# Order of the reflections, of the residual sum and of two late pieces in a fused attention, expert and rotation kernel

## The chip, the cores and the metric

One Trainium2 chip, and on it one core. The core has five engines that run beside each other, each through its own list of instructions in order: TensorE (PE in the profile; its weight loads are PEld), VectorE (DVE), ScalarE (ACT), GpSimd (POOL) and SyncE (SP). Work passes between them by semaphores. The kernel uses SP and POOL to issue most of its DMA transfers, and an issue waits in the list of its engine like any other instruction; a sequencer's own part of an engine is marked with a q (SPq, POOLq).

The metric is the device time of one launch in microseconds. Before the change three runs gave 720.19, 721.65 and 724.29 us; the median, 721.65 us, is what a ratio is taken to.

## The reference

The input is x of 4 batches of 512 tokens with 288 channels, and one condition vector for each batch. All arithmetic is float32.

```python
mod = silu(c) @ w_adaln + b_adaln           # six vectors of 288 for each batch
h   = layernorm(x) * (1 + sc_msa) + sh_msa
o   = attention(h, 16 heads of 18)          # 512 x 512 scores in each head
x   = x + g_msa * (o @ w_proj + b_proj)
xn  = layernorm(x) * (1 + sc_mlp) + sh_mlp
cw  = softmax weights of the best 2 of 4 experts, by xn @ w_gate
moe = sum_e cw[e] * (gelu(xn @ w1[e] + b1[e]) @ w2[e] + b2[e])      # 1152 hidden
x   = x + g_mlp * moe
U, _ = qr(P)                                # P: 288 x 64
R   = expm(A(c))                            # a 64 x 64 rotation for each batch
out = x + ((x @ U) @ R - x @ U) @ U.T
```

## The kernel before, in words

Tokens lie on the 128 partitions, so a batch is 4 tiles of 128 tokens. The program has two large stages and a short end.

**Attention, in 64 steps.** The heads go in groups of four; a step is one group and one tile of 128 keys. The groups of all batches are numbered n = 0 to 15 (batch n // 4, group g = n % 4), and a step is written (g, t). In each step TensorE makes the scores `z` (L1780), ScalarE takes their exponential `es` (L1789), and TensorE multiplies the exponentials of the step before with the values into `av` (L1798). All the rest of the work is cut into pieces, and a dictionary `steps[g, t]` names by hand the pieces that follow the scores of each step. The list `beside` gives one more piece to each step, from the matrices of the rotation. The pieces that matter here:

- *Normalisation of a group n*, in four pieces: `first` copies `av` to `oraw` on ScalarE (L1815) and has SP bring the softmax sums to `den` (L1818); `reciprocals` inverts them on VectorE (L1824) and has SP write them to memory as `rdr` (L1826); `spread` has SP load them back, one row for 32 partitions, into the tile `oT` (L1834); `divide` multiplies `oraw` by `oT` on VectorE (L1840). Below, "den(14)" and the like mean such a piece of group 14.
- *`merge` of a batch*, one piece for each token tile: TensorE multiplies `oT` by the projection into `po` (L1856), VectorE multiplies it by a gate into `og` (L1865), and GpSimd adds `og` to the tile of x, `xs` (L1866). It runs during the next batch, in the steps (1,1) and (1,2).
- *`statistics`* (L1167 to L1176): mean and variance of each token on VectorE, and then on GpSimd the factor `rs`, the power -1/2 of variance + eps, and `ms` = -mean * rs. `normalized` applies both on ScalarE (`xh`, L1184).
- *`routing` of a batch* starts after its merge, in the step (1,3) of the next batch, with the statistics. Its pieces are `norm` (`xh` on ScalarE), `logits0` and `logits1` (VectorE: modulation, L1882 and L1883, and the gate logits, L1930), `top` and `choices` (the best two experts, VectorE), `ratio` (an exponential, ScalarE) and `gates_`. After batches 1 and 3, that is when half of the tokens are known, the pieces `ranks_of`, `by_rank` and `slots_of` give each token its slots, and GpSimd writes the rows there by 16 indirect transfers (`slots`, L2119), which are issued one after the other between other pieces.
- *A column*: one of the 64 reflections of the QR of P. All of it is VectorE work: some 20 small instructions which each need the one before (L1541 to L1605), so about 5 us. A piece `column` takes the next of the list `chain` (a first step, 64 columns, and `ws`, which ends the list). The columns are told apart below by the width that they still have: the column of 267, of 266 and so on.

**Experts, in 108 steps.** The tokens are taken in two halves, each with four passes (one expert each). A pass loads its rows from the slots (`xg`), turns them, multiplies them by the first weights (`ph`, L2443 and L2456), takes the gelu (`hm`, L2465), multiplies by the second weights (`pe`, L2503), and has GpSimd scatter the result into `chosen` (L2519). The list `rest` gives one piece to each step. It opens with `last_merge`, the division of the groups 14 and 15 and the merge of batch 3; then come the routing of batch 3 and the columns that are left; later `turned` and the other pieces that make the basis U (`pwt`, L1625, is the first TensorE work that needs the last column), and the sums of the first half. At the second piece of each pass the program also issues the next pass's `xg` on SP (L2175 to L2180), and it does so ahead of the piece of that step.

**The end.** The sums of the second half, the projection on U, the rotation and the store, in a pipeline over pairs of tiles.

What sets the order: each engine's list is the order in which the Python program issues its instructions, and SP's and POOL's transfers stand in these lists too. PSUM tiles for side work come in turn from three buffers in the attention stage (two of `ps_m`, one of `third`), and from two after it; a piece that is late in emptying its buffer holds up the third, or second, piece after it on TensorE.

Of the kernel before, what the change touches and what calls it, by code (L numbers as in the profile page):

```python
# [10 lines left out]
F32 = mybir.dt.float32  # L11
I32 = mybir.dt.int32
AF = mybir.ActivationFunctionType
ALU = mybir.AluOpType
# [4 lines left out]
P = 128  # L19
HD = 18  # L20
HQ = 32
LN_EPS = 1e-6
# [791 lines left out]
def fast_path(  # L814
# [24 lines left out]
    nc = tc.nc  # L839
    B, N, C = x.shape  # L840
    CC = C // 3
    NK = 3
    NT = N // P
# [97 lines left out]
    def bank(shape, name):  # L941

        banks[0] += 1
        if third and banks[0] % 3 == 0:
            return third[0].tile(shape, F32, tag="n", name=name)
        return ps_m.tile(shape, F32, tag="m", name=name)
# [3 lines left out]
    small = ctx.enter_context(tc.tile_pool(name="small", bufs=4))  # L950
# [6 lines left out]
    with ExitStack() as s1:  # L957
# [204 lines left out]
        def statistics(b, which):  # L1162
            st = small.tile([P, NT, 6], F32, tag="st", name=f"st{which}{b}")
            mv = small.tile([P, NT, 2], F32, tag="mv", name=f"mv{which}{b}")
            rs = small.tile([P, NT], F32, tag="rs", name=f"rs{which}{b}")
            for t in range(NT):
                nc.vector.bn_stats(st[:, t, :], xs[:, b * NT + t, :])  # L1167
                nc.vector.bn_aggr(mv[:, t, :], st[:, t, :])
            nc.gpsimd.tensor_scalar_add(rs, mv[:, :, 1], LN_EPS)
            nc.gpsimd.tensor_tensor(rs, rs, neghalf, ALU.pow)  # L1170
            if (b, which) != (0, 0):

                ms = small.tile([P, NT], F32, tag="ms", name=f"ms{which}{b}")
                nc.gpsimd.tensor_tensor(ms, mv[:, :, 0], rs, ALU.mult)
                nc.gpsimd.tensor_scalar_mul(ms, ms, -1.0)
                return ms, rs  # L1176
            return mv, rs

# [673 lines left out]
        def merge(b):  # L1852
            def tile_of(t):
                po = bank([P, C], f"po{b}{t}")
                for g in range(NG):
                    nc.tensor.matmul(  # L1856
                        po,
                        oTs[b][:, g, ts(t, P)],
                        wp[:, g, :],
                        start=(g == 0),  # L1860
                        stop=(g == NG - 1),
                    )
                xt = xs[:, b * NT + t, :]
                og = small.tile([P, C], F32, tag="og", name=f"og{b}{t}", bufs=2)
                nc.vector.tensor_mul(og, po, gates[:, 0, b, :])  # L1865
                nc.gpsimd.tensor_tensor(xt, xt, og, ALU.add)  # L1866

            return [lambda t=t: tile_of(t) for t in range(NT)]

        def route(b):  # L1870

            xr = rt.tile([P, NT, ROW], F32, tag="xr", name=f"xr{b}", bufs=B // HALVES)
            parts = statistics(b, 1)

            xhs_ = []

            def norm():
                xhs_.append(normalized(b, 1, *parts))

            def modulated(t):  # L1880
                xh = xhs_[0]
                nc.vector.tensor_mul(xh[:, t, :], xh[:, t, :], modrow[:, 1, b, :])  # L1882
                nc.vector.tensor_add(xr[:, t, :C], xh[:, t, :], modrow[:, 0, b, :])  # L1883

            def with_logits(i, logits):
                for t in range(i * NT // 2, (i + 1) * NT // 2):
                    modulated(t)
                logits()

            chosen_ = choose(b, xr)  # L1890
            for i in range(2):
                chosen_[i] = lambda i=i, logits=chosen_[i]: with_logits(i, logits)
            return [norm] + chosen_
# [5 lines left out]
        def scatter_next():  # L1899
            if scatters:  # L1900
                scatters.pop(0)()
# [242 lines left out]
        NN = B * NG  # L2144
        norm, turns, values = begin(0)
# [103 lines left out]
        chain, basis = triangular()  # L2249
        held, divides, late = [], {}, []  # L2250

        def gather_oldest():
            n, t, es = held.pop(0)
            gather(n, t, es)
            if t == NT - 1:
                first, *divides[n] = normalize(n)
                first()

        def divide(n):
            if n in divides:  # L2260
                divides[n].pop(0)()
# [4 lines left out]
        def also(step, *pieces):  # L2266
            steps[step].extend(pieces)

        def routing(b):
            def start():  # L2270
                norm, logits0, logits1, top, choices, ratio, gates_, *end = route(b)
                also((2, 1), norm)
                also((2, 2), logits0)
                also((2, 3), logits1)
                if b == B - 2:

                    also((3, 0), top, choices)
                    also((3, 3), ratio)
                    late.append(gates_)
                    return  # L2280
                also((3, 0), top, choices)
                also((3, 1), ratio)
                also((3, 2), gates_, *end[:1])
                also((3, 3), *end[1:])

            return start
# [14 lines left out]
        for n in range(NN):  # L2301
            b, g = divmod(n, NG)
            if g == 0:
                steps = {(i, t): [] for i in range(NG) for t in range(NT)}
                for i in range(NG):
                    also((i, 0), lambda n=n + i - 2: divide(n))
                    for t in (2, 3):
                        also((i, t), lambda n=n + i - 1: divide(n))
                if b > 0:
                    merges = merge(b - 1)  # L2310
                    also((1, 1), *merges[:2])
                    also((1, 2), *merges[2:])
                    also((1, 3), routing(b - 1))
                else:

                    for step in ((1, 0), (1, 3), (2, 1), (2, 3)):
                        also(step, column)
                if b + 1 < B:
                    also((1, 1), beginning(b + 1))
                if b > 0:  # L2320
                    also((0, 2), column)
                if b == B - 1:
                    also((2, 0), column)
                for step in ((0, 0), (0, 1), (0, 3), (3, 1)):
                    also(step, column)
                also((2, 3), lambda b=b: residual(b))
            if g == 0:
                queue = nc.gpsimd if b else nc.sync
                products, sends = project(b, 1, queue)
                also((0, 0), products[0])  # L2330
                also((0, 1), products[1])
                also((0, 2), *sends[:3])
                also((0, 3), *sends[3:5])
                also((1, 0), *sends[5:])
                products, sends = project(b, 2, queue)
                also((0, 2), *products)
                also((0, 3), sends[0])
                also((1, 1), sends[1])
            if g == 3 and b + 1 < B:
                products, sends = project(b + 1, 0)  # L2340
                also((3, 0), products[0])
                also((3, 1), products[1])
                also((3, 2), *sends[:4])
                also((3, 3), *sends[4:])
            if n == NN - 1:
                wx = wxs[0]
                weights = [expert_weights(0)]
                takes = take_slots(0, xg0)
                also((3, 2), *takes[:3])
                also((3, 3), *takes[3:])  # L2350
            for t in range(NT):
                if (n, t) == (NN - 2, 0):

                    xg0 = load_slots(0, a2, "hT", 1, nc.gpsimd)
                held.append((n, t, weigh(n, t)))
                if len(held) > 1:
                    gather_oldest()
                for piece in steps[g, t]:
                    piece()
                if beside:  # L2360
                    beside.pop(0)()
                scatter_next()
                if g in (0, 1, 3):
                    scatter_next()
        while held:
            gather_oldest()
        for piece in beside:
            piece()
        last_merge = [
            lambda: (divide(NN - 2), divide(NN - 1)),  # L2370
            lambda: divide(NN - 1),
            column,
            lambda: divide(NN - 1),
            None,
            *merge(B - 1),
            *late,
        ]
# [4 lines left out]
    with ExitStack() as s2:  # L2382
# [148 lines left out]
        class Finish:  # L2531
# [6 lines left out]
            late = []  # L2538
# [137 lines left out]


        ROUTING = 13
        rest = [*last_merge, last_routing] + [column] * (len(chain) - 4)
        ends = basis + [None, all_fit, subspace, None] + [  # L2680
            lambda n=n: early(n) for n in range(PAIRS + 1)
        ] + [None] * 4
        steps = HALVES * (E * NF + SLOTS // P)
# [131 lines left out]
```

## Time and profile before

The profiled execution took 724.75 us, 3.10 us more than the median of the three runs; its span from the first to the last instruction is 723.0 us.

| engine | busy, us | share of the span | instructions |
|---|---|---|---|
| PE (TensorE matmul) | 674.6 | 93% | 3563 |
| PEld (weight load) | 391.4 | 54% | 3563 |
| DVE (VectorE) | 485.3 | 67% | 2204 |
| ACT (ScalarE) | 290.2 | 40% | 465 |
| POOL (GpSimd) | 223.3 | 31% | 350 |

| stretch of the span, us | PE busy | DVE busy | POOL busy | granted clock of TensorE |
|---|---|---|---|---|
| 0 to 60 | 52.83 | 35.42 | 21.80 | 1.00 |
| 60 to 120 | 52.83 | 38.66 | 31.78 | 0.91 |
| 120 to 180 | 56.63 | 44.61 | 15.61 | 0.97 |
| 180 to 240 | 56.03 | 48.24 | 17.39 | 1.00 |
| 240 to 300 | 52.84 | 40.40 | 32.84 | 0.97 |
| 300 to 360 | 51.77 | 28.66 | 11.77 | 0.89 |
| 360 to 420 | 60.00 | 48.90 | 19.43 | 1.00 |
| 420 to 600 (mean of 60) | 59.85 | 53.29 | 18.71 | 1.00 |
| 600 to 660 | 58.13 | 13.66 | 12.59 | 1.00 |
| 660 to 720 | 53.95 | 26.85 | 3.97 | 0.94 |

How to read it: the attention stage ends near 319 us, and the expert stage runs from there to 691 us. TensorE is hardly ever idle in the expert stage; its idle time, 48.4 us in all, lies in the attention stage, about the change of stage, and at both ends. A busy share is an average, so the question for each edit is which single wait of TensorE it touches.

### The profile page before, as it was taken

Reading aid. Unit: us, or ns where it says so; the run is one execution under the profiler, and the core shown is the slowest. Engines: PE = TensorE matmul, PEld = TensorE weight load, DVE = VectorE, ACT = ScalarE, POOL = GpSimd, SP = SyncE. Lnnn points to the kernel's source line nnn. Section 1 sums busy time; section 2 is a strip of 40 time slices with the busy share of each in tenths; the row PEclk is TensorE's granted clock in tenths of the full one; section 3 lists DMA queues with packets and bytes.
Section 4 is the critical chain, followed back from the end, with each engine's and each line's share of the span. In section 5 each row is a group of like instructions: output and inputs, shape, how many; then the busy total and the mean of one; then the engine's idle time right before and its main releaser. Section 6 shows DMA issues by size and latency. Waiting matters only on the chain. (4 is left out here: it accounts for less than half of the span.)

```text
span 723.0 us, 11477 instructions
## 1 busy us (share of the span) xinstructions
PE 674.6 (93%) x3563; PEld 391.4 (54%) x3563; DVE 485.3 (67%) x2204; ACT 290.2 (40%) x465; POOL 223.3 (31%) x350
## 2 busy tenths in 40 slices
PE   6999699999998999596999999999999999999986
PEld 5423333333343434143677776777667676667753
DVE  5473868696868883873178788988888886005244
ACT  3566455575547554462224323223232332222231
POOL 3055922601252346720142163622204032121110
PEclk9999899999999999799899999999999999999997
DMA  9488812001100123425143543255343053206043
GB/s 208 137 242 205 283 46 53 21 17 46 49 20 17 54 79 92 138 55 156 60 120 68 171 121 121 73 153 173 75 145 90 12 174 76 90 22 217 18 157 122
DMA packets 70528, 75.47 MB, mean 104 GB/s; under 512 B 33452, under 2 KB 57746, under 8 KB 70458
## 3 DMA queue, kind: packets, MB, share of 16 engines
q1 hardware_dynamic: 60166, 47.78, 24.1%
q0 software_dynamic: 9792, 26.45, 12.1%
q10 hardware_dynamic: 500, 0.42, 0.3%
q8 instruction: 30, 0.49, 0.3%
q14 instruction: 40, 0.33, 0.2%
HBM read 52.13 MB, written 18.23 MB: 97 GB/s over the span
## 5 line engine op out<-in xcount | busy, mean ns | idle before, releaser
L2503 PE MATMUL pe<-w2s,hm 128*128 128x288 f32 (+1 forms) x648 | 163.7, 408 | 0.0
L2443 PE MATMUL ph<-xgT,w1s 128*128 128x288 f32 (+2 forms) x576 | 152.9, 416 | 0.4
L1789 ACT ACTIVATE es<-z 128x1024 f32<-128x1024 f32 x128 | 123.9, 1020 | 69.8 <-PE z L1780 68.1
L2503 PEld LDWEIGHTS pe<-w2s,hm 128*128 128x128 f32 (+1 forms) x648 | 118.7, 187 | 31.5 <-issue 2.3
L2443 PEld LDWEIGHTS ph<-xgT,w1s 128*128 128x128 f32 x576 | 106.8, 191 | 40.5 <-issue 11.4
L2465 ACT ACTIVATE hm<-ph,b1r 128x576 f32<-128x576 f32 (+2 forms) x72 | 49.9, 738 | 140.0 <-PE ph L2456 121.6
L1780 PE MATMUL z<-qk 32*128 32x512 f32 x512 | 90.7, 650 | 14.1 <-ACT es L1789 14.1
L1798 PE MATMUL av<-es,vt 128*32 128x512 f32 x512 | 70.8, 626 | 0.0
L2518 POOL TENSOR_TENSOR y<-y,gb 128x288 f32<-128x288 f32 x32 | 26.1, 816 | 126.6 <-ACT y L2517 126.5
L1780 PEld LDWEIGHTS z<-qk 32*128 32x128 f32 x512 | 27.3, 186 | 58.9 <-ACT es L1789 43.4
L2517 ACT ACTIVATE y<-pe,weight 128x288 f32<-128x288 f32 x32 | 16.0, 501 | 104.2 <-PE pe L2503 100.8
L1742 PE MATMUL pq<-hT,wqk 96*126 96x512 f32 (+3 forms) x120 | 56.5, 608 | 0.0
L2519 POOL DMA_INDIRECT chosen<-y,place x36 | 36.7, 1019 | 53.0 <-DVE y L2515 34.3
L1562 DVE SCALAR_TENSOR_TENSOR q<-q 64x1 f32<-64x1 f32 (+1 forms) x192 | 44.3, 231 | 7.0
L2119 POOL DMA_INDIRECT slots<-xr,where x32 | 32.6, 1017 | 47.4 <-DMA slots<-xr,where 38.8
L1754 POOL DMA_DIRECT2D qk<-row x42 | 21.6, 519 | 72.5 <-ACT row L1749 72.4
L1856 PE MATMUL po<-wp,oT 128*128 128x288 f32 x128 | 35.0, 421 | 9.2 <-DVE oT L1840 9.2
L1573 DVE STREAM_SHUFFLE wj<-pt 32x288 f32<-32x288 f32 (+47 forms) x96 | 42.1, 439 | 0.7
L1742 PEld LDWEIGHTS pq<-hT,wqk 96*126 96x126 f32 (+3 forms) x120 | 20.7, 183 | 33.8 <-issue 28.9
L1798 PEld LDWEIGHTS av<-es,vt 128*32 128x32 f32 x512 | 10.2, 109 | 48.8 <-issue 40.3
L1856 PEld LDWEIGHTS po<-wp,oT 128*128 128x128 f32 x128 | 23.5, 191 | 22.4 <-DVE oT L1840 10.6
L1840 DVE TENSOR_TENSOR oT<-oraw,oT 128x512 f32<-128x512 f32 x16 | 11.0, 689 | 34.3 <-DMA oT<-rdr 28.0
(281 smaller groups left out, 895.6 us busy)
## 6 DMA issues: line engine op xcount, KB each, us to landing
w2s<-in_w_dram SPq DMA_DIRECT2D x8, 1296.0 KB
w1s<-in_w_dram SPq DMA_DIRECT2D x8, 1152.0 KB
slots<-empty POOLq DMA_DIRECT2D x36, 148.0 KB
oT<-rdr SPq DMA_DIRECT2D x64, 64.0 KB
qk<-row POOLq DMA_DIRECT2D x42, 72.0 KB
yc<-chosen SPq DMA_DIRECT2D x4, 576.0 KB
out_dram<-xs SPq DMA_DIRECT2D x8, 288.0 KB
wr<-in_wrT_dram POOLq DMA_DIRECT2D x4, 567.0 KB
```

Source lines behind the costliest of these rows:

```text
L1562: nc.vector.scalar_tensor_tensor(s, u, part, s, ALU.mult, ALU.add)
L1573: nc.vector.stream_shuffle(wj[o : o + HQ, j:], pt[o0 : o0 + HQ, j:], [j % HQ] * HQ)
L1742: nc.tensor.matmul(pq[:n], wqk[:rows, k, item, :n], hT[:rows, k, :], start=(k == 0), stop=(k == NK - 1),)
L1780: nc.tensor.matmul(zs[c // 2][:, c % 2, :], qk[ts(c, HQ), 1, ts(t, P)], qk[ts(c, HQ), 0, :], start=True, stop=True,)
L1789: nc.scalar.activation(e, z, AF.Exp, scale=SCALE)
L1798: nc.tensor.matmul(avs[n][ts(c, HQ), :], vts[b % 2][:, t, 4 * g + c, :], es[c // 2][:, c % 2, :], start=(t == 0), stop=(t == NT - 1),)
L1856: nc.tensor.matmul(po, oTs[b][:, g, ts(t, P)], wp[:, g, :], start=(g == 0), stop=(g == NG - 1),)
L2119: nc.gpsimd.indirect_dma_start(out=slots[h], out_offset=bass.IndirectOffsetOnAxis(ap=where[:, i, t : t + 1], axis=0), in_=xrs[t // NT][:, ...
L2443: nc.tensor.matmul(ph[:, j, :SB], w1s[:, k, ts(f, P)], xgT[:, k, ts(j, SB)], start=(k == 0), stop=False,)
L2465: nc.scalar.activation(hm[:, f, : CAPS[r]].rearrange("p (j s) -> p j s", j=NB), ph[:, :, :SB], AF.Gelu_apprx_tanh, bias=b1r[:, h, r, f : f ...
L2503: nc.tensor.matmul(po[ts(m, rows), :], slots_[:, f, :], w[:, f, :], start=(f == 0), stop=(f == NF - 1),)
L2519: nc.gpsimd.indirect_dma_start(out=chosen[h], out_offset=bass.IndirectOffsetOnAxis(ap=place[:, t : t + 1], axis=0), in_=y, in_offset=None, ...
```

## The change

- The columns of a step are issued last in it, after the step's other pieces and after the piece of `beside`. Before, they stood among the other pieces, and ahead of `beside`.
- The merge's sum `xs + og` is made on VectorE and no longer on GpSimd.
- `statistics`: variance + eps and the negated mean are made on VectorE, the power and one product stay on GpSimd; before, all four were on GpSimd.
- The routing of batch 2, which runs in the steps of batch 3: `norm` moves from the step (2,1) to (2,2), `logits0` from (2,2) to (2,3), `logits1` from (2,3) to (3,0), and `top` with `choices` from (3,0) to (3,1); `ratio` stays in (3,3).
- `last_merge`, the first ten pieces of the expert stage: the three pieces with divisions move from the places 0, 1 and 3 to the places 1, 2 and 3; the column of place 2 moves to place 0, and a second column takes place 4, which was empty. One column fewer is left for later.

```diff
-            nc.gpsimd.tensor_scalar_add(rs, mv[:, :, 1], LN_EPS)
+            nc.vector.tensor_scalar_add(rs, mv[:, :, 1], LN_EPS)
+            if (b, which) != (0, 0):
+                ms = small.tile([P, NT], F32, tag="ms", name=f"ms{which}{b}")
+                nc.vector.tensor_scalar_mul(ms, mv[:, :, 0], -1.0)
             nc.gpsimd.tensor_tensor(rs, rs, neghalf, ALU.pow)
             if (b, which) != (0, 0):
-                ms = small.tile([P, NT], F32, tag="ms", name=f"ms{which}{b}")
-                nc.gpsimd.tensor_tensor(ms, mv[:, :, 0], rs, ALU.mult)
-                nc.gpsimd.tensor_scalar_mul(ms, ms, -1.0)
+                nc.gpsimd.tensor_tensor(ms, ms, rs, ALU.mult)
                 return ms, rs
...
                 nc.vector.tensor_mul(og, po, gates[:, 0, b, :])
-                nc.gpsimd.tensor_tensor(xt, xt, og, ALU.add)
+                nc.vector.tensor_add(xt, xt, og)
...
                 norm, logits0, logits1, top, choices, ratio, gates_, *end = route(b)
+                if b == B - 2:
+                    also((2, 2), norm)
+                    also((2, 3), logits0)
+                    also((3, 0), logits1)
+                    also((3, 1), top, choices)
+                    also((3, 3), ratio)
+                    late.append(gates_)
+                    return
                 also((2, 1), norm)
                 also((2, 2), logits0)
                 also((2, 3), logits1)
-                if b == B - 2:
-                    also((3, 0), top, choices)
-                    also((3, 3), ratio)
-                    late.append(gates_)
-                    return
...
+                columns = [piece for piece in steps[g, t] if piece is column]
                 for piece in steps[g, t]:
-                    piece()
+                    if piece is not column:
+                        piece()
                 if beside:
                     beside.pop(0)()
+                for piece in columns:
+                    piece()
                 scatter_next()
...
         last_merge = [
+            column,
             lambda: (divide(NN - 2), divide(NN - 1)),
             lambda: divide(NN - 1),
+            lambda: divide(NN - 1),
             column,
-            lambda: divide(NN - 1),
-            None,
             *merge(B - 1),
             *late,
         ]
...
-        rest = [*last_merge, last_routing] + [column] * (len(chain) - 4)
+        rest = [*last_merge, last_routing] + [column] * (len(chain) - 5)
```

In the two built programs TensorE's instructions stand in the same order. ScalarE's list differs in one place: `xh` of batch 2 stands after the next two exponentials. SP's differs in one place: `rdr` of group 15, which stood before the six transfers of the second pass's `xg`, stands after them. VectorE's and GpSimd's lists differ where the edits above say so.

## The prediction

> **What bounds the kernel now.** I read the page's slices first, then TensorE's timeline with the waits ahead of its groups, then the timelines of the engines that those waits name.
>
> ```profile
> PE   6999699999998999596999999999999999999986
> DVE  5473868696868883873178788988888886005244
> PEclk9999899999999999799899999999999999999997
> ```
>
> A slice is 18.1 us. TensorE is full from slice 20 to the end of the expert stage, so that stage can't be shortened by order. What can be won are single waits. Of those in TensorE's timeline, these could be touched by the change:
>
> ```profile
> 80.13 1.09 PE L1205 MATMUL pt<-ident,xh 128*96 128x128 f32 x4 [5.65 <-DVE brs L1323]
> ...
> 301.41 2.98 PE L1780 MATMUL z<-qk 32*128 32x512 f32 x8 [8.22 <-ACT es L1789]
> ...
> 334.80 1.72 PE L1856 MATMUL po<-wp,oT 128*128 128x288 f32 x6
> 343.15 1.33 PE L1856 MATMUL po<-wp,oT 128*128 128x288 f32 x2 [6.62 <-DVE oT L1840]
> ...
> 608.76 0.37 PE L1625 MATMUL pwt<-ident,pt 64*96 64x64 f32 x3 [0.81 <-DVE pt L1620]
> ```
>
> Together 21.3 us of waiting. Two merges also wait 1.18 and 1.39 us for `oT`. VectorE's list ahead of those two keeps its order, so they stay. The 8.22 us come through ScalarE from GpSimd:
>
> ```profile
> 294.90 0.98 POOL L2119 DMA_INDIRECT slots<-xr,where  x1 [1.78 <-DMA slots<-xr,where]
> ...
> 295.96 0.23 POOL L1169 TENSOR_SCALAR rs<-mv 128x4 f32<-128x4 f32 x1
> ...
> 297.69 0.54 POOL L1175 TENSOR_SCALAR ms<-ms 128x4 f32<-128x4 f32 x1
> ...
> 298.27 2.18 ACT L1184 ACTIVATE xh<-xs,ms,rs 128x288 f32<-128x288 f32 x4 [7.26 <-POOL ms L1175]
> ```
>
> GpSimd finishes the last of 16 row transfers and only then makes `ms`; ScalarE waits with `xh` in hand and the exponentials queue behind it. The 6.62 us come from SP's list:
>
> ```profile
> 321.59 0.35 SPq L1826 DMA_DIRECT2D rdr<-den  x1
> 323.85 1.72 SPq L1834 DMA_DIRECT2D oT<-rdr  x4
> 325.67 2.41 SPq L1818 DMA_DIRECT2D den<-oraw  x4
> 328.97 0.41 SPq L930 DMA_DIRECT2D w2s<-in_w_dram  x1
> 329.51 0.57 SPq L1826 DMA_DIRECT2D rdr<-den  x1
> 330.17 0.38 SPq L2175 DMA_DIRECT2D xg<-slots  x1
> 330.60 7.60 SPq L2177 DMA_DIRECT2D xg<-slots  x4
> 338.25 0.53 SPq L2180 DMA_DIRECT2D xg<-slots  x1
> 338.88 1.86 SPq L1834 DMA_DIRECT2D oT<-rdr  x4
> ```
>
> The load that group 15's division needs stands behind `xg`. Its four loads take 7.60 us to issue, against 2.15 us in the next two passes; the `w2s` of 1296 KB went just before. VectorE's `oT` starts at 342.40, 3.52 us after the last issue's start.
>
> **Columns last in a step.** No work is added; only VectorE's order changes. The largest move is at the start: `modrows`, which waits for TensorE until 37.14, now stands ahead of the first column, which ran in that wait (23.63 to 29.40, 5.77 us). VectorE stands idle there and has the column to do later. The statistics of batch 1 ended at 52.1, so now near 57.9. VectorE's wait of 3.67 us for `den` until 55.79 covers part, and den(0) comes 2.6 us late (58.4). Behind it is its `rdr`, issued at 56.07 and landed only when SP issues the next at 65.84, the DMA engines being full (share 0.84 to 1.05) from 48 to 64. GpSimd's `wgd`, issued at 58.55, landed by 66.31 too. So I take 0 for it; without that cover 2.6. `xh` of batch 1 starts 1.2 us later, and the 5.65 us at 80.13, which VectorE's own column sets, hide that. Elsewhere the pieces that pass a column are the rotation's, and the list of TensorE's waits names none of them but `brs`, which keeps its place: 0.
>
> **The merge's sum and the statistics.** GpSimd loses 16 additions of 796 ns. VectorE gains 16; the nearest row, 128x288 from two SBUF tiles, is 0.46 us, so 1.8 us for a batch, beside its waits for `po` (4.9 us in the first merge). Two small operations of 0.17 us for each statistics come on top. In batch 2 VectorE no longer waits for GpSimd (7.0 us before `og`, 4.2 us before the statistics): they end at 286.2, not 292.4. That isn't what `xh` waits for. GpSimd still has all the row transfers first, each after its predecessor has landed, 2.8 us apart. From 282.40 four remain, about 285.7, 288.5, 291.3 and 294.1, against 294.90; then one power (1.05) and one product (0.20) in place of four operations. So `ms` is ready at 296.4, not 298.2: 1.8 us earlier. At least 0.9 (two small operations gone), at most 4.1 (the 3.16 us of four additions gone whole as well).
>
> **Routing a step later.** The next exponentials pass `xh` on ScalarE. So the scores that now start at 301.41 start at 293.2, and those after them wait for `xh` and one exponential: 296.4 + 2.18 + 1.02 = 299.6, where they now start at 306.2. With a slow restart TensorE is 4 to 5 us earlier at 311, and at `po` (334.8 now 330).
>
> That is kept only if oT(15) comes earlier too. VectorE can start the logits with the first `xh`, 0.6 us after `ms`: 297.0 against 298.97, so 2.0 earlier. From there to den(14) its work is the same (logits, oT(13), `top`, `choices`, column of 266), 22.36 us: 319.3 against 321.33. In it six operations of 0.45 us take 1.04 beside GpSimd's additions at 305.5 to 310.2; those move along, so I keep them (without them another 3.5 us).
>
> **The last division.** SP: spread(14) at 321.8, den(15) until 326.0, `w2s` at 326.95, and `xg` directly, since `rdr`(15), which waited for VectorE ahead of it, now stands behind it. `xg` ends 9.8 us after `w2s` (336.75) or 2.75 us earlier than now (336.05); I take 336.4. Then comes what was hidden under `xg` before: `rdr`(15) has to land before its load may be issued. From its issue to the next one's start five rows give 1.43, 1.44, 2.16, 2.26 and 2.72 us (261.25, 298.86, 240.29, 321.59, 79.02); the middle is 2.16. So the load at 338.6 and `oT` at 338.6 + 3.52 = 342.1, against 342.40: a gain of 0.3. TensorE's earlier arrival turns into a longer wait, about 11 us.
>
> A rule that speaks against this edit: the Trainium skill, "DMA: Bandwidth & Descriptors", section "Queues, rings and completion order", says that on each DMA engine a ring's descriptors are consumed in ring order, so `rdr`(15) would start behind all of `xg`. In this trace the load that stood there until now arrived 3.52 us after its issue's start, against 3.42 for group 14's, so the ring was empty by then. By the row the sum is the -1.1 below. By the rule, with all 0.98 MB of `xg` still to pass at the 213 to 389 GB/s that the DMA engines moved from 330 to 336, it would be 2.5 to 4.6 us more: +1.4 to +3.5, an estimate.
>
> **The second column** of `last_merge` follows oT(15) on VectorE (342.8 to 347.9), so the first `og` starts 3.4 us later. `po` has two buffers, and the third `po` starts at 352.75: covered by 4 us; if not, up to 3.4. VectorE then has one column fewer (about 4.9 us) in a stretch, 364 to 608, where it waits only 3.7, 2.6 and 0.2 us; the last column no longer holds `pwt`: -0.8.
>
> **Sum**: 0 - 0.3 - 0.8 = -1.1 us; span 721.9, the profiled time 724.75 becoming 723.65. The profiled run is 3.1 us above the median, so I take the difference from the median: 720.5 us.
>
> **Rivals.** *A, the second wait shrinks too.* If `xg` issues as in the later passes (0.4 + 2.15 + 0.8 = 3.4 us), `rdr`(15) goes at 330.9 and `oT` starts at 330.9 + 2.0 + 3.5 = 336.4: 6.0 earlier, with 0.8 more: 714.8. For it: nothing but SP and transfers stand in that stretch. Against: `w2s` stays just ahead, and 2.3 MB have to pass (0.98 MB of them `xg`). Half of it is possible, also through fewer slow logits.
>
> *B, `rdr`(15) is stuck behind `xg`.* Of the same transfer, the longest wait for landing is 9.8 us (56.07 to 65.84, behind other loads). At that price `oT` starts at 336.45 + 9.8 + 3.5 = 349.75, 7.35 late; less 0.8: 728.2. It makes a loss of the whole from a wait of 3.3 us, and a visible one from 6.9. For it: the list's order. Against: the 3.52 above.
>
> **How the numbers follow.** A measurement here can't tell less than about 0.5% (3.6 us) from no change. Forecast 0.52, its own range 717.5 to 723.2 (xg, landing, `ms`, and 2.6 of the start); A in part or whole 0.30; B, with the start's 2.6, 0.18. Likeliest 720.5. From 714.0, under A, to 725.5, which leaves out most of B. Faster 0.30, same 0.52, slower 0.18.
>
> **What would show it.** Right: the 8.22 us gone or below 4.5; `ms` near 296; the wait at `po` near 11 and ending near 343; `rdr`(15) after L2180 on SP; no wait at `pwt`; the wait near 80 kept. Wrong: `po` resumed before 340 (A) or after 345 (B), or a wait of the first 80 us moved by over 2 us.

## The result, and the profile after

The changed kernel takes 729.98 us (median of four runs, 729.28 to 731.63), the kernel before 722.97 us beside it (four runs, 720.19 to 725.66). The ratio is 1.0101, with a 95% interval of 1.0054 to 1.0147; six later runs gave 1.0079 (1.0059 to 1.0099). Ratios here and below are estimates from the undisturbed runs of both kernels, not the quotient of two medians. The forecast was 720.5 us, from 714.0 to 725.5: the change made the kernel slower, and the time lies outside the range. The profiled execution of the changed kernel took 729.48 us with a span of 727.8 us, which is 4.8 us above the span of 723.0 us shown ahead.

The slices of the page, 18.2 us each, look almost alike; what differs lies between slices 4 and 20, the attention stage and the change of stage, and in the last slice:

```profile
PE   6998898999988997997799999999999999999995
PEclk9998999989999998999799999999999999999997
```

The reading begins with TensorE's timeline, whose columns are start, duration, engine, line, operation and, in brackets, the wait ahead of it and what ended it. The third merge had no wait in the kernel before, which is why no line of it stands ahead of the prediction:

```profile
272.34 4.15 PE L1856 MATMUL po<-wp,oT 128*128 128x288 f32 x16
```

These are lines of the changed kernel, the third merge first, and then those that answer to the waits shown of before:

```profile
277.41 1.72 PE L1857 MATMUL po<-wp,oT 128*128 128x288 f32 x6
283.72 5.17 PE L1857 MATMUL po<-wp,oT 128*128 128x288 f32 x10 [4.59 <-DVE oT L1841]
...
305.55 1.41 PE L1781 MATMUL z<-qk 32*128 32x512 f32 x8
...
339.34 1.72 PE L1857 MATMUL po<-wp,oT 128*128 128x288 f32 x6
350.46 1.33 PE L1857 MATMUL po<-wp,oT 128*128 128x288 f32 x2 [9.40 <-DVE oT L1841]
...
614.90 0.37 PE L1626 MATMUL pwt<-ident,pt 64*96 64x64 f32 x3
```

Two of the waits to be won are indeed gone, the 8.22 us after the third merge and the 0.81 us at `pwt`. But all three merges wait longer in this execution. Put beside the same groups of the kernel before, in us, the places left out above among them:

| place on TensorE | wait before | wait after | start after minus before |
|---|---|---|---|
| `pt` near 80 | 5.65 | 2.71 | -0.34 |
| first merge, second part of `po` | 1.18 | 2.43 | +0.60 |
| second merge, second part of `po` | 1.39 | 2.75 | +3.38 |
| third merge: scores of the step behind it | 0 | 4.59 (at `po`) | +12.40 |
| scores that waited 8.22 (301.41, now 305.55) | 8.22 | 0 | +4.14 |
| first `ph` of the expert stage | 0 | 1.00 | +4.31 |
| last merge, resumed | 6.62 | 9.40 | +7.31 |
| `pwt` | 0.81 | 0 | +6.14 |

So the wait of 8 us is gone, and more than that had been lost just ahead of it. TensorE comes to the second merge 2.03 us late and to the third 5.07 us late; the largest step is at the third merge, 7.3 us in one place. At the end 1.3 of the 6.14 us are regained: the last products behind a wait took 10.58 us at a granted clock of 0.68 in the trace before (from 705.03, after 1.75 us of waiting) and 9.05 us at 0.81 in this one (from 711.33, after 1.91 us). The next section of the trace to read is VectorE's, since `oT` is what TensorE waits for there. VectorE's timeline of the changed kernel, from the division of group 10, in the first step of the last batch, to the `oT` of group 11 that the third merge needs (a line at L1545 ends a column, here that of 268; L1488 is the copy of a squaring of the rotation):

```profile
254.05 0.69 DVE L1841 TENSOR_TENSOR oT<-oraw,oT 128x512 f32<-128x512 f32 x1
259.56 0.30 DVE L1488 COPY_PREDICATED XY<-need,psq 128x128 f32<-128x128 int32 x1 [4.81 <-PE psq L1438]
...
282.57 0.49 DVE L1545 SCALAR_TENSOR_TENSOR pt<-wj,uf,pt 64x268 f32<-64x268 f32 x1
282.99 0.68 DVE L1841 TENSOR_TENSOR oT<-oraw,oT 128x512 f32<-128x512 f32 x1
```

And the same stretch of the kernel before:

```profile
248.98 0.69 DVE L1840 TENSOR_TENSOR oT<-oraw,oT 128x512 f32<-128x512 f32 x1
...
254.67 0.49 DVE L1544 SCALAR_TENSOR_TENSOR pt<-wj,uf,pt 64x271 f32<-64x271 f32 x1
255.08 0.28 DVE L1487 COPY_PREDICATED XY<-need,psq 128x128 f32<-128x128 int32 x1
...
272.72 0.68 DVE L1840 TENSOR_TENSOR oT<-oraw,oT 128x512 f32<-128x512 f32 x1
```

The same work stands in both. Before, the column of 271 ran first, from 249.6 to 255.2, and the squaring's copy behind it waited for nothing. After, the copy stands first: VectorE stops for 4.81 us with a column ready behind it, and then has four columns to do, 271 to 268, without a gap until `oT`. From `oT` to `oT` it is 23.74 us before and 28.94 us after: 5.20 us more, 4.81 of them the wait. What the copy waits for is a product that TensorE makes late in that step, behind the scores, the product with the values and a projection of 2.84 us:

```profile
256.05 2.84 PE L1743 MATMUL pq<-hT,wqk 97*126 97x512 f32 x6
258.82 0.68 PE L1438 MATMUL psq<-XY 64*64 64x64 f32 x16
```

The price on TensorE is 7.3 us, not 4.6, since the clock is down when it resumes. Busy time and granted clock (the third number from the end) of the ten products of `po` in the three merges, changed kernel (the counts take in neighbouring instructions):

```profile
126.07:128.76 2.69, 2.69 (x14) 1.88 (x14) 0.92 (x2) 0.00 (x0) 0.00 (x0) 1.00 0.04 8
203.05:207.43 4.38, 4.38 (x14) 2.92 (x14) 2.07 (x7) 0.00 (x0) 0.00 (x0) 0.61 0.00 0
283.72:288.89 5.17, 5.17 (x14) 3.23 (x14) 1.07 (x3) 0.00 (x0) 2.69 (x4) 0.50 0.29 90
```

Ten products take 2.69 us at the full clock and 5.17 us at half of it. So 4.59 us of wait and 2.48 us of a restart at half the clock make 7.1 of the 7.3 us.

### The profile page after: what moved, and what is told of

Read it like the earlier page. It is cut to its first block, busy times and chain, and to the rows that moved or that the text cites. A ratio compares the mean times of both kernels' runs of the same rounds, so it can differ in the third digit from the quotient of the medians.

```text
span 727.8 us, 11485 instructions
## 1 busy us (share of the span) xinstructions
PE 678.3 (93%) x3563; PEld 391.4 (54%) x3563; DVE 490.4 (67%) x2235; ACT 290.2 (40%) x465; POOL 205.9 (28%) x319
## 5 line engine op out<-in xcount | busy, mean ns | idle before, releaser
L1857 PE MATMUL po<-wp,oT 128*128 128x288 f32 x128 | 39.4, 459 | 19.2 <-DVE oT L1841 19.2
L1857 PEld LDWEIGHTS po<-wp,oT 128*128 128x128 f32 x128 | 25.8, 210 | 34.1 <-DVE oT L1841 21.0
```

Of the source, the lines that this page charges most:

```text
L1857: nc.tensor.matmul(po, oTs[b][:, g, ts(t, P)], wp[:, g, :], start=(g == 0), stop=(g == NG - 1),)
```

## The experiments

Three theories stood against each other. *C*: the columns' new place lets VectorE stand idle at the rotation's pieces. *V*: the sums and statistics that VectorE was given make `oT` late. *L*: the new order of the last divisions costs the time. Each kernel was run six to twelve times, beside 29 to 35 runs of the kernel before; ratios are to it. The first four share a chip, all others another one, so a comparison across these two groups goes by the ratios alone.

**1. The columns back in their old place, all else as changed.**

```diff
-                columns = [piece for piece in steps[g, t] if piece is column]
                 for piece in steps[g, t]:
-                    if piece is not column:
-                        piece()
+                    piece()
                 if beside:
                     beside.pop(0)()
-                for piece in columns:
-                    piece()
```

> The changed kernel with the columns of a step back in their old place; all other parts of the change stay. Theory C (VectorE now stands idle at the rotation's pieces, waiting for TensorE's products, where a column used to run, and the merges' oT come late): TensorE's waits at the three merges are back near 1.2, 1.4 and 0 us, VectorE's waits at the rotation's copies (L1488) are back from 5.8 us to below 1, and the time is 719 to 724 us, ratio to before 0.996 to 1.002. Theory V (the sums and statistics added to VectorE make oT late) and theory L (the new order of the last divisions costs the time): it stays at 728 to 731, ratio 1.008 to 1.012.

Measured: 720.45 us, ratio 0.9954 (0.9929 to 0.9979), the time as expected and the ratio a little better. The merges wait 1.59, 1.52 and 0 us, and VectorE's wait at L1488 is 1.0 us in all. The third merge in this trace:

```profile
272.97 4.15 PE L1857 MATMUL po<-wp,oT 128*128 128x288 f32 x16
```

The rest of the change is a gain, and the loss is the columns' place: C holds. V and L fall as causes of the loss.

**2. The columns last, and nothing else of the change.** The edit is the same block, put into the kernel before.

> The kernel before with the columns issued last in a step, and nothing else of the change. Theory C: the merges' waits are near 2.4, 2.7 and 4.6 us as in the changed kernel, TensorE is 10 to 13 us late at the step (2,0) of the last batch, the wait of 8.22 us after it takes a part of that, and the time is 727 to 733 us, ratio 1.006 to 1.014. Theories V and L: 721 to 724, ratio 0.998 to 1.002.

Measured: 727.19 us, ratio 1.0053 (1.0026 to 1.0081), the time at the lower end of what was expected and the ratio just under it. The merges wait 2.50, 2.74 and 4.62 us, and TensorE is 11.34 us late behind the third. Then comes the place of the 8.22 us, of which 0.89 us are left (the scores start at 305.63). TensorE arrives late at a wait that it would have had anyway, and 7.1 us of the delay vanish in it. This is why the parts don't add up: moving the columns costs 0.5% alone, and some 1.2% within the change (from 0.9954 or 0.9962 to 1.0079), where the routing's new step has removed most of the wait that would have hidden it. The traces say the same: beside experiment 1 the changed kernel is 11.76 us late behind the third merge, and still 9.68 us late at the scores behind `xh` (308.80 against 299.12).

**3. The columns behind the step's own pieces, but ahead of `beside`.**

```diff
-                if beside:
-                    beside.pop(0)()
                 for piece in columns:
                     piece()
+                if beside:
+                    beside.pop(0)()
```

> The changed kernel with the columns behind the step's own pieces but ahead of the piece of beside, as in the kernel before. Theory C in its narrow form (the rotation's pieces of beside are the ones that wait): VectorE's wait of 4.8 us at L1488 is gone, the third merge's wait falls from 4.6 us to below 1.5, and the time is 720 to 725 us. If it is the step's own pieces ahead of the columns that cost it (modulation, products, sums of the merge), it stays at 727 to 731.

Measured: 721.14 us, ratio 0.9962 (0.9939 to 0.9986), as good as with the columns back. VectorE's waits at L1488 are 1.0 us, the third merge doesn't wait. So it isn't the step's own pieces that must not pass the columns, but the piece of `beside`: the narrow form of C. (`modrows` at the start is such a piece as well, so this edit takes back that part of the move too.) VectorE's waits by cause say it in two views, first the changed kernel, then this one (total, times, longest):

```profile
DVE XY L1488 <- PE psq L1438: 5.8, 2, 4.8
```

```profile
DVE XY L1488 <- PE psq L1438: 1.0, 1, 1.0
```

With the two other groups that take a product of the rotation from TensorE and waited over 1 us (L1454 and L1476), it is 10.0 us in the one and 2.5 us in the other; of this, L1454 alone varies from 1.1 to 2.8 us among the kernels with the columns in their old place.

**4. The columns back, and the old `last_merge` too.** Beside the edit of the first experiment:

```diff
         last_merge = [
-            column,
             lambda: (divide(NN - 2), divide(NN - 1)),
             lambda: divide(NN - 1),
-            lambda: divide(NN - 1),
             column,
+            lambda: divide(NN - 1),
+            None,
```

> As the kernel with the columns back in their old place, and the last merge's pieces in their old order too: only the sums and statistics on VectorE and the routing a step later are left of the change. Theory C with the prediction's sum: within 2 us of the kernel with the columns back, 719 to 724 us, VectorE's last oT near 342. Theory L: 2 us or more faster than that kernel. Theory V: 727 to 731, both kernels alike.

Measured: 717.87 us, ratio 0.9923 (0.9891 to 0.9955), 0.3% below experiment 1. Theory L is true in the small, by what the traces show: `oT` of group 15 starts at 338.87 here and at 341.08 in experiment 1, and TensorE's last wait ends at 339.61 against 341.83. The two ratios' intervals overlap, so the loss rests on the traces, 2.2 us at this place, more than on the times.

**5 and 6. The sums and statistics alone; the routing a step later alone.** Each is the hunk of the change, put into the kernel before.

> The kernel before with the merge's sums and the two small operations of the statistics on VectorE, and nothing else of the change. By the prediction's steps (ms 1.8 us earlier, the exponentials still behind xh): the wait of 8.22 us falls to about 6.4, VectorE's waits for GpSimd's sums (7.0 and 4.2 us) are gone, the merges' waits at oT keep 1.2, 1.4 and 0 us, and the time is 720 to 723 us when before is at 723, ratio 0.996 to 1.000. Theory V: the merges' waits grow by 1 us or more each and the ratio is above 1.004.

Measured: ratio 0.9958 (0.9926 to 0.9990). VectorE's waits for GpSimd's sums are gone, and the wait of 8.22 us is down to 5.14 us. That isn't the gain that was expected, though: in this trace TensorE comes 6.0 us late to the place (299.19 against 293.19), the last row transfer is issued at 298.81 and not at 294.90, and the scores start at 304.33, later than before. What can be read is the distance from the start of that issue to `xh`, 2.38 us against 3.37 before, 1.0 us less. V falls once more by the ratio: VectorE's added work costs nothing that shows. (The first merge waited 3.36 us in this trace, but also 3.57 us in that of experiment 6, which has no such sums.)

> The kernel before with the third batch's routing one step later and nothing else of the change. By the prediction's steps, with ms at 298.2 as in the kernel before: the scores at 301.41 start without waiting near 293.2, those after them wait for xh and one exponential until 298.2 + 3.2 = 301.4, where they started at 306.2: 4 to 5 us earlier there, and the last oT up to 2 us earlier. Ratio 0.993 to 0.999. If the gain needs the sums on VectorE as well, it is within 0.2% of before.

Measured: ratio 0.9962 (0.9935 to 0.9988). The scores that waited 8.22 us don't wait, those after them wait 5.44 us for `xh`, as the steps of the prediction have it. They start at 304.40 and not at the 301.4 expected, and the last `oT` at 345.39, 3.0 us later than before instead of up to 2 earlier: TensorE was 3.4 us late at the third merge in this trace. By the ratios each of the two parts is worth about 0.4% alone, and 0.8% together (experiment 4). The profiled executions don't show it, with spans of 723.3 and 722.6 us against 723.0, so where these gains arise is read from experiments 1 and 4, not from these two.

**7. The load for group 15's division ahead of the second pass's row transfers.** Experiment 4 with:

```diff
-            lambda: (divide(NN - 2), divide(NN - 1)),
-            lambda: divide(NN - 1),
+            lambda: (divide(NN - 2), divide(NN - 1), divide(NN - 1)),
             column,
             lambda: divide(NN - 1),
             None,
+            None,
```

> The kernel with the columns back and the old last merge (the fastest so far), with the load that group 15's division needs issued ahead of the second pass's six row transfers on SP, not behind them. If that list sets the last oT, oT starts near 326.7 + 2.1 + 3.5 = 332.3 us instead of 338.87, TensorE's last wait of 1.6 us at po is gone, and the time is 1 to 3 us below that kernel, ratio to before 0.988 to 0.991. If the wait was not on the path, or the row transfers are missed where they end later, the ratio stays at 0.992 or goes up.

Measured: ratio 0.9902 (0.9868 to 0.9936), TensorE no longer waits at the last `po`; it comes there only at 342.31 in this trace, and in experiment 12, with the same edit, it waits 4.53 us. And the steps of the expectation were wrong: `rdr` needs 5.90 us and not 2.1 from its issue to the next one's start, so `oT` starts 9.6 us behind `rdr`'s issue, not 5.6. The 2.1 us came from transfers that no weights stood directly ahead of; here `w2s` was issued half a microsecond earlier (see experiment 12).

**8. The old order in one step alone, the first of the last batch.** In the changed kernel the block moves a column only where `(b, g, t) != (B - 1, 0, 0)`.

> The changed kernel with the old order in one step alone, the first of the last batch, where VectorE waits 4.8 us at L1488 ahead of the column; all other steps keep the columns last. Theory C: that wait is gone, the third merge's wait at po falls from 4.6 to below 1 us, TensorE is 5 to 8 us earlier at the step (2,0) of the last batch, and the time falls by 4 to 8 us, ratio to before 1.000 to 1.005. If the delay comes from many steps, it stays above 1.007.

Measured: ratio 1.0036 (1.0008 to 1.0063), in the expected range, but not for the expected reason. The copy at 258.00 no longer waits, and the next squaring, two steps on, does:

```profile
268.48 0.30 DVE L1488 COPY_PREDICATED XY<-need,psq 128x128 f32<-128x128 int32 x1 [4.11 <-PE psq L1438]
```

The third merge still waits 3.89 us. The wait has moved to the next place where a product stands ahead of a column. That fits a VectorE which runs ahead of TensorE until it has lost these 4 to 5 us once, wherever. The span of this trace is only 1.4 us below that of the changed kernel's first trace and 2.3 below its second (experiment 11). The ratio fell by 0.4%, some 3 us, but the two intervals overlap.

**9 and 10. The old order in the first four steps of the last batch; and the converse.** Conditions `(b, g) != (B - 1, 0)` and `(b, g) == (B - 1, 0)` for moving a column. Experiment 11 is the changed kernel again, on the same chip.

> The changed kernel with the old order in the first four steps of the last batch, (0,0) to (0,3); all other steps keep the columns last. One step put back only let the wait come up at the next square, two steps on. Theory C: with all four put back VectorE waits less than 1 us at L1488 in these steps, the third merge's wait at po falls from 4.6 to below 1.5 us, the first two keep about 2.4 and 2.7, and the time is 0.5 to 1.0% below the changed kernel of the same call, ratio to before 0.999 to 1.004. If the rest of the loss comes from the first two merges and the start alone, it stays within 0.2% of the changed kernel.

> The converse: all parts of the change, the columns in their old place everywhere but in the first four steps of the last batch, where they are last. Theory C: VectorE waits 4 to 5 us at L1488 and the third merge 3.5 to 5 us at po, with the first two merges at 1.2 to 1.9; the time is 0.4 to 1.0% above the kernel with all columns back (0.9954), ratio to before 0.999 to 1.005.

> The changed kernel itself, as the measure for its neighbours: ratio to before between the bounds of the first measurement, 1.005 to 1.015.

Measured: the changed kernel again 1.0079 (1.0059 to 1.0099); with the four steps back 1.0011 (0.9991 to 1.0030); with only these four new 1.0005 (0.9982 to 1.0028), against 0.9954 with none, that one measured on the other chip. The four steps cost 0.7% when taken away from the one end and 0.5% when added at the other. In experiment 9 VectorE waits nowhere at L1488 in these steps, and the third merge not at all; the first two wait 4.25 and 2.76 us. In the traces it is one place: the time from the scores ahead of the third merge to those behind it falls by 7.33 us in experiment 9, against the changed kernel, and grows by 7.25 us in experiment 10, against experiment 1. The first view is of experiment 9; in that of experiment 10 VectorE's copy has the wait again, and `po` of the third merge then waits 4.52 us for `oT` (the first two merges wait 2.42 and 1.50 us):

```profile
257.76 0.28 DVE L1488 COPY_PREDICATED XY<-need,psq 128x128 f32<-128x128 int32 x1
```

```profile
256.08 0.30 DVE L1488 COPY_PREDICATED XY<-need,psq 128x128 f32<-128x128 int32 x1 [4.81 <-PE psq L1438]
```

What is left in experiment 9 above experiment 3, 0.5%, comes from the other steps. In the traces most of it lies ahead of the third merge, that is at the start and the first two merges: there TensorE is already 1.97 us later than in experiment 3, and 2.66 us at the last merge. It wasn't split further, and can't be read from one trace: the first merge's wait varies from 1.08 to 3.57 us among the profiled executions that have the columns in their old place, and was 2.43 us in the changed kernel's first trace and 1.30 us in its second.

**12. The columns as in experiment 3 and the last load as in experiment 7.**

> The columns behind the step's own pieces but ahead of beside, and group 15's load ahead of the second pass's row transfers. In the profile of the first of these two edits TensorE arrives at the last merge at 331.5 and resumes at 341.4; in that of the second the load's issue starts 5.9 us after its rdr, since the w2s transfer is still under way, and oT 3.5 us behind. So oT starts near 326.95 + 5.9 + 3.5 = 336.4, TensorE resumes near 337 and the time is about 4 us below the kernel with the first edit alone (0.9962): ratio 0.988 to 0.992, the fastest of all. If other waits take the place, it stays at 0.992 to 0.996.

Measured: ratio 0.9933 (0.9913 to 0.9954). `oT` starts at 336.12 and TensorE resumes at 336.86, as expected, and the profiled execution is the shortest of all, with a span of 714.1 us. But the time isn't the 4 us below experiment 3 that this was to give: the ratio lies in the second range that was expected, that of other waits taking the place. It isn't below that of experiment 4 or 7; the three can't be told apart by their intervals, and all three beat both kernels, by 0.7 to 1.0% against the kernel before. SP's list shows the price of the early load:

```profile
325.49 0.41 SPq L930 DMA_DIRECT2D w2s<-in_w_dram  x1
326.02 0.66 SPq L1827 DMA_DIRECT2D rdr<-den  x1
332.65 1.71 SPq L1835 DMA_DIRECT2D oT<-rdr  x4
```

`rdr` has landed after 6.63 us, behind 1296 KB of `w2s`.

## Why the prediction was wrong

**The step that failed** is the last sentence on the columns: "Elsewhere the pieces that pass a column are the rotation's, and the list of TensorE's waits names none of them but `brs` [...]: 0", and with it "VectorE's list ahead of those two keeps its order, so they stay" on the merges. The list doesn't keep its order ahead of the merges: pieces of the rotation that take a product pass a column in the steps (0,0) and (0,2), squarings in the last batch. And the third merge, which had no wait to show and cost the most, wasn't looked at. The argument on the columns looked for TensorE waiting on those pieces. The other direction wasn't looked at: VectorE waits for TensorE in them, and a column that ran first had been the cover. Before, VectorE waited 0.3 us at the squarings, which says that the cover was there, not that there was nothing to cover. In its place the runs showed about 1.2% within the change, some 8.6 us, which is also what lies between the spans of experiment 3 (719.2) and of the changed kernel (727.8), 7.8 of them there by `pwt`; 0.5 to 0.7% of it lie ahead of the third merge alone (experiments 1, 3, 9, 10, 11).

The prediction did apply the right question at the start of the kernel, where `modrows` passes a column; it worked out den(0) at 58.4 (`rdr` was issued at 58.61), and the cover by the transfers (the load after it was issued at 65.31, before it was 65.84). That part cost nothing at `den`, as said. The delay of `xh` was put at 1.2 us; the scores at 62 came 1.15 us late, and by 71 it was 2.6 us. The wait near 80 hid it, falling from 5.65 to 2.71 us. In the changed kernel's second trace `brs` came 1.84 us later than before and the wait was 5.42 us, so the start doesn't end alike in each execution.

**Most other steps held**, as experiment 1 shows, which is the change without the columns' move. `ms`, put at 296.4: `xh` starts at 295.98. Scores at 293.2 and 299.6: 293.75 and 299.12. den(14) at 319.3: 319.05. `rdr`(15) behind `xg`, 2.16 us to land: 3.20, 2.08 in experiment 3 and 1.96 in the changed kernel. oT(15) at 342.1: 341.08. The wait at `pwt`: gone. For these steps the sum was -1.1 us from 721.65; experiment 1 gave a ratio of 0.9954, which is -3.3 us. In its trace TensorE is 1.39 us ahead of before at `pwt` (607.37 against 608.76), close to the sum. The rest of the 3.1 us between the spans arises in the last products, which no step of the sum speaks of: 10.58 us at a granted clock of 0.68 before, 8.62 us at 1.00 in experiment 1.

The term on the last division, a gain of 0.3, had the wrong sign in what the edit itself does. With the sums and the routing moved, oT(15) comes at 338.87 in the old order and at 341.08 in the new one (experiments 4 and 1): `rdr`(15) behind `xg` has to land where nothing hides it any more. The prediction held the new order against 342.40, the old order without the two other parts.

**A wait that wasn't on the list.** TensorE was to be at `po` at 330 and came at 336.59 in experiment 1. The first product of the expert stage waits 3.47 us there for `xgT`, which in ScalarE's list stands behind the exponential of `ratio`; that one waits for VectorE, since `top` now runs a step later and behind a column. The sixteen products behind that wait took 6.49 us, against 4.57 before, so the two make 5.4 of the 6.6 us. The same in experiment 4, in ScalarE's timeline, where the first product then waits 3.47 us as well:

```profile
318.36 0.21 ACT L1964 ACTIVATE g<-g 128x4 f32<-128x4 f32 x1 [3.95 <-DVE g L1960]
```

It was hidden in experiment 1 by the wait for oT(15), which shrank to 3.52 us. In experiment 3, where the columns stand behind `top`, the first product starts 3.2 us earlier (315.54), and the last merge waits 8.20 us instead: nothing won.

**The rivals.** Rival B's 728.2 us is close to the result, and its mechanism is not what happened: behind `xg`, `rdr`(15) landed in 1.96 us, as SP's list of the changed kernel shows:

```profile
337.14 6.55 SPq L2178 DMA_DIRECT2D xg<-slots  x4
343.74 0.53 SPq L2181 DMA_DIRECT2D xg<-slots  x1
344.36 0.47 SPq L1827 DMA_DIRECT2D rdr<-den  x1
346.32 1.72 SPq L1835 DMA_DIRECT2D oT<-rdr  x4
```

TensorE's 9.40 us at the last merge are long because VectorE came to den(14) at 328.98 instead of 321.33. The mechanism exists in another place: directly behind `w2s` the same transfer took 5.90 and 6.63 us until the next issue (experiments 7 and 12). The rule cited from the Trainium skill, "DMA: Bandwidth & Descriptors", section "Queues, rings and completion order", that a ring's descriptors are consumed in order, would allow that; the runs don't tell ring order from DMA engines that are merely full. Rival A's mechanism, an `xg` that issues as quickly as in the later passes, came true in small part: its four loads took 6.55 us in the changed kernel and 6.25 to 6.68 us in experiments 1, 3 and 4, against 7.60 before and the 2.15 assumed. The second wait did shrink with the old `last_merge`, where the load's `rdr` lands while `xg` is being issued: 1.08 us are left of 6.62 in experiment 4. Of the difference 3.5 us come from `oT` and 2.0 us from TensorE, which arrives later.

## What to carry to other kernels

Before a piece is moved ahead of another on an engine, ask not only who waits for it, but what it waits for, and what has been running in that wait until now: a short wait in the trace of before can mean a long one that is covered. Long independent work, as the columns are, belongs behind the start of what it is to cover and ahead of the piece that takes the product. And two edits that act on one wait don't add: the 8.22 us could hide the late merge or be won by the routing, not both.

## What the runs showed of the hardware

After a wait of TensorE in a merge, the ten products behind it took 2.69 us at a granted clock of 1.00, 3.91 to 4.38 us at 0.61 to 0.67, or 5.17 us at 0.50 to 0.51. The length of the wait alone doesn't say which: 2.37 us in experiment 8 were followed by 0.62, and 2.76 us in experiment 9 by 1.00; 4.25 us in experiment 9 by 0.61, and 3.89 us in experiment 8 by 0.51. The second merge alone has 2.74 us followed by 0.67 in experiment 2, 2.74 us by 0.50 in experiment 11, and the 2.76 us by 1.00:

```profile
203.30:208.47 5.17, 5.17 (x14) 3.24 (x14) 2.07 (x7) 0.00 (x0) 0.00 (x0) 0.50 0.00 0
202.35:205.04 2.69, 2.69 (x14) 1.88 (x14) 2.08 (x7) 0.00 (x0) 0.00 (x0) 1.00 0.00 0
```

The first of these lines is of experiment 11, the second of experiment 9. So a wait of 2.4 to 4.6 us in a merge cost between nothing and 2.5 us on top of itself. At the end of the kernel it happened behind shorter waits too: 1.75 us before were followed by 0.68 over the last 10.58 us of products, and 1.96 us in experiment 1 by 1.00. The Trainium skill, "TensorE: Matmul & The Clock Gate", section "What's actually happening", has the clock fall after at least one idle window of about 3.4 us that runs free of the kernel. A free-running window fits waits of like length that end differently; the falls after 2.37 us and 1.75 us lie below the page's figure, and here the measurement decides.
